# The last two steps of a two-half recurrence: a gate of one half over all four column tiles, and two x units for the second half first

## The chip, the cores and the metric

The kernel runs on one core of one Trainium2 chip. The metric is the device time in microseconds. TensorE (PE in the profile; its weight loads are PEld) has a 128 x 128 array that this kernel uses as four column tiles of 32 columns each; the four tiles work side by side on separate products. VectorE (DVE), ScalarE (ACT), GpSimd (POOL) and SyncE (SP, which here issues DMA transfers) run beside it, each in the order of its own list of instructions, and wait for each other through semaphores.

## The reference

A gated recurrence over T = 128 steps for a batch of 64, with 512 inputs and a state of 512, whose output is added to the input:

```python
comb = concat([x_t, h])
z = sigmoid(comb @ Wz + bz)
r = sigmoid(comb @ Wr + br)
h_cand = tanh(concat([x_t, r * h]) @ Wh + bh)
h_new = (1 - z) * h + z * h_cand
h = tanh(h_new @ Wp + bp) if (t + 1) % 4 == 0 and t < T - 1 else h_new
out[:, t] = x[:, t] + h_new
```

All data is fp32. The part `x_t @ W` does not depend on the state and can be worked out at any time before its step; the part `h @ W` and everything behind it is a chain from step to step.

## The kernel before

**Halves and tiles.** The batch is two halves of 32 (`h` = 0, 1). A gate's 512 results are split by columns in two parts of 256. Half 0 keeps column tiles 0 and 1, half 1 tiles 2 and 3; a tile holds the 32 batches of its half in its 32 columns' partitions and 256 results along the free dimension. The state enters turned, as weights of 128 x 32. `gate` (L255) makes the recurrent product of one gate for one half: K = 4 parts of the 512-long sum, and in `products` (L244, the matmul at L246) one fp32 matmul of 128 x 256 for each of the two tiles. One k of one half and one unit of x work of one half have the same number of columns (256 on each tile of the pair).

**A step** (`half`, one coroutine per half) has gates R, Z and H, and after each fourth step but the last a gate P (the propagation, with `wp`). After R the sigmoid goes to `r_` (`crossed`, L276 to L281: two ACT instructions of 64 rows, since the two parts of a gate lie in two halves of a bank), DVE multiplies by the state (L918) and turns the result (L284): that is the weights of gate H. After Z come sigmoid and `keep` (L941); after H the tanh (L281), z times it (L980), the new state (L993) and its turning (L284): that is the weights of the next R. `r_` (L198) is the last quarter of PSUM bank `scratch_r`.

**Banks.** Three PSUM banks (`rec`) hold the gates; five (`scratch_q`, `_r`, `_a`, `_x`, `_y`) take the x products. `seed` (L439) copies x product and bias into a gate's bank with ACT (L442) before the recurrent product adds to it. For most steps the x products come from a fast matrix scheme with 192-column matmuls (`batch`, L529) whose sums GpSimd puts together; for the first steps and the last two from `plain` (L505), a direct product of twelve units a step, to which DVE adds the bias (`add_bias`, L480 and L483).

**Order.** x work stands in one queue of units (`put`, L454). `fill(n, h)` (L460) runs the next n units of the queue for one half; each half goes through the whole queue at its own place. A unit that writes a bank waits, for half 0, until half 1 has gone past the last unit whose result is read out of that bank; the reading itself (`end`) is issued when half 1 runs the unit. How many units stand after gate Z, after gate H and after gate P of a step is written in `PLACES`, `HEAD` and `TAIL` (L669 to L676, the last by step). The two coroutines are merged by a clock that counts columns (L1019 to L1031): the half that is behind goes next, and half 1 begins 700 columns later (`LAG`).

**The end.** x + h_new is put into `xr` by GpSimd (L876) and sent by SP, every four steps in eight transfers (L886); at step T - 2 the eight transfers hold three steps. The last step adds by DVE (L951, L983); half 0 goes out in one transfer on SP (L985) and half 1 in four, two on SP and two on ACT's queue (L990). `late(t)` names the steps (T - 7 and from T - 5) in which the two halves of Z are activated apart.

Of the kernel before, what the change touches and what calls it, by code (L numbers as in the profile page):

```python
# [13 lines left out]
ALU = mybir.AluOpType  # L14
# [4 lines left out]
def kernel(  # L19
# [417 lines left out]
                G[2 * q + b] = cp[q][:, :, b]  # L437

    def seed(i, t, h):  # L439
        if t < T:  # L440
            rows = slice(None) if i == Z else ts(h, 2 * V)
            nc.scalar.copy(  # L442
                gate_ps(i, h)[rows].rearrange("p d (c n) -> p d c n", c=C),
                G[t][rows, :, :, i, :].rearrange("p c d n -> p d c n"),
            )
# [6 lines left out]
    reader = {}  # L452

    def put(units):  # L454
        for unit, cols, bank, end, read in units:
            queue.append((unit, cols, reader.get(bank, -1), end))
            for b in read:
                reader[b] = len(queue) - 1

    def fill(n, h):  # L460
        for _ in range(n):
            if place[h] == len(queue):
                return
            unit, cols, after, end = queue[place[h]]
            while h == 0 and after >= place[1]:
                yield 0
            unit(h)
            yield cols
            place[h] += 1
            if h == 1 and end is not None:  # L470
                end()

    def banks(t):
        first, second = scratch[:2] if t % 2 == 0 else scratch[2:4]
        if t < 2:
            return first[:, : S * J], second[:, : S * J], scratch[4][:, ts(t, S * J)]
        rooms = (first[:, : S * J], first[:, S * J :], second[:, : S * J])
        return (rooms[0], rooms[2], rooms[1]) if t == T - 1 else rooms

    def add_bias(t, gates):  # L480
        new_cp(t // 2)
# [7 lines left out]
    def plain_unit(t, e, k, start, end=None, gates=()):  # L489
        g, i = divmod(t, Q4)  # L490
        bank = (q_bank, q_bank, r_bank) if t % 2 == 0 else (a_bank, a_bank, x_banks[0])
        if t == T - 1:
            bank = (a_bank, x_banks[0], a_bank)
        second = H_ if t in (1, T - 1) else None if t == 0 else Z
        return (
            lambda h: product(
                banks(t)[e], h, xT[g][:, i], wx[:, :, e, :], k, start and e != second
            ),
            S * J,
            bank[e],  # L500
            end,
            {bank[e] for e in gates},
        )
# [14 lines left out]
        ]  # L518

    MB = {}

# [5 lines left out]
    def batch(n, ms):  # L529
        def runs(ps):  # L530
            return ps.rearrange("p m h (g u) -> p m (h g) u", g=3)

        def unit(h, ps, m, j, e, start):
            g, i = ms[m]
            x_, w_ = terms(i)[e]
            right = factor(w_, j)
            products(
                ps[:, m].rearrange("p d (g u) -> p d g u", g=3),
                h,
                lhs(g, x_, j)[:, ts(h, V)],  # L540
                lambda c: right[:, c::2],
                start and m == 0 and e == 0,
            )
# [36 lines left out]
        def end_q2():  # L580
            nonlocal q2
            q2 = copied("cq", "cq2", q_ps)
            nc.vector.tensor_add(blocks(1, 1), runs(q_ps[:, :nm]), runs(T2[what][:, :nm]))  # L583

        def end_r2():
            nc.vector.tensor_add(blocks(0, 1), runs(r_ps[:, :nm]), runs(q2[:, :nm]))
            nc.vector.tensor_add(blocks(1, 0), runs(x_ps[:, :nm]), runs(q2[:, :nm]))  # L587

        seq = []
        for ps, bank, j, start, end, read in (  # L590
            (a_ps, a_bank, 2, True, None, ()),
            (x_ps, x_bank, 7, True, end_x, (x_bank,)),
            (q_ps, q_bank, 1, True, end_q, (q_bank,)),
            (r_ps, r_bank, 5, True, end_r, (r_bank, a_bank)),
            (x_ps, x_bank, 4, False, None, ()),
            (q_ps, q_bank, 6, False, end_q2, (q_bank,)),
            (r_ps, r_bank, 3, False, end_r2, (r_bank, x_bank)),
        ):
            us = units(ps, j, start)
            seq += [(u, 3 * J // 2, bank, None, ()) for u in us[:-1]]  # L600
            seq.append((us[-1], 3 * J // 2, bank, end, read))
        return seq

    M = {}
# [59 lines left out]
    def pair_right(a, p1, x_, g=1):  # L664
# [96 lines left out]
    def begin(t):  # L761
# [54 lines left out]
    def behind_step(t, duo, u, h_new):  # L816
# [78 lines left out]
        if duo >= 0:  # L895
            if u == 3:
                load_xs(odd + 2)
            elif u == 7:
                load_xs(even + 4)

    def half(h):

        for t in range(T):
# [4 lines left out]
            places = HEAD.get(t) or TAIL.get(t) or PLACES[u]  # L908
            if h == 0:
                begin(t)  # L910
            h_old, hT = state[t]

            yield from gate(R, h, hT, wh[R])
# [20 lines left out]

            def gate_z(part, halves, h_old=h_old, z_=z_, keep=keep):
                for i in halves:
                    crossed(z_[:, i, :], i, Z, AF.Sigmoid, not last)
                kept = keep[:, part, :], z_[:, part, :], h_old[:, part, :]
                if last:
                    kept = plain_order(kept[0]), plain_order(kept[1]), state_order(kept[2])  # L940
                nc.vector.scalar_tensor_tensor(  # L941
                    out=kept[0],
                    in0=kept[1],
# [2 lines left out]
                    op0=ALU.subtract,  # L946
                    op1=ALU.mult,
                )
                if last:
                    o = xr[g][:, j, part, :]  # L950
                    nc.vector.tensor_sub(o, o, keep[:, part, :])  # L951

            if h == 1:
                if late(t):
                    gate_z(0, (0,))
                    if last:
                        gate_z(1, (1,))
                else:
                    gate_z(slice(0, S), range(S))
                join(t, duo, u, 1)  # L960
# [15 lines left out]
            if late(t) and h == 1 and not last:  # L976
                gate_z(1, (1,))
            crossed(cand[:, h, :], h, H_, AF.Tanh, not last)
            c = z_[:, h, :]
            nc.vector.tensor_mul(c, cand[:, h, :], c)  # L980
            if last:
                o = xr[g][:, j, h, :]
                nc.vector.tensor_add(o, c, o)  # L983
                if h == 0:
                    nc.sync.dma_start(  # L985
                        out=out[ts(h, V), t, :].rearrange("b (q n) -> q b n", q=NQ), in_=o
                    )
                else:
                    for q in (0, 2, 1, 3):
                        both_queues[q // 2].dma_start(out=out[ts(h, V), t, ts(q, J)], in_=o[part(q)])  # L990
                return
            hT = new_turned("hT", "hT", t)
            nc.vector.tensor_sub(h_new[:, h, :], c, keep[:, h, :])  # L993
            turn(hT[:, h, :], h_new[:, h, :])
            if prop:
                nc.scalar.copy(gate_ps(P_, h)[ts(h, 2 * V)], bias_p[ts(h, 2 * V)])
            elif not late(t + 1):
# [73 lines left out]
```

## Time and profile before

| what | value |
|---|---|
| median of three runs | 1259.13 us (1259.06 to 1259.54) |
| the profiled execution's own time | 1258.66 us |
| its span, first to last instruction | 1256.6 us |
| granted TensorE clock | 1.000 |
| TensorE busy | 1248.4 us (99%), 25952 MATMULs |
| weight loads busy | 1155.6 us (92%) |
| VectorE, ScalarE, GpSimd busy | 809.1, 836.3, 909.7 us (64%, 67%, 72%) |
| HBM | 40.38 MB read, 16.78 MB written, 45 GB/s |

In the rows below, a group is named by its line, engine and operation, then out <- in by the program's names, the shapes and the number of instructions. In a timeline a row has the start in us, the length in us and, in brackets, the idle time of the engine before it and what ended it. The records of matmuls overlap: a record is longer than the distance to the next matmul on the same tile, and the busy time of TensorE counts the stretch that at least one record covers. Each fp32 matmul is recorded as two MATMULs and two LDWEIGHTS.

### The profile page before, as it was taken

Reading aid. Unit: us, or ns where it says so; the run is one execution under the profiler, and the core shown is the slowest. Engines: PE = TensorE matmul, PEld = TensorE weight load, DVE = VectorE, ACT = ScalarE, POOL = GpSimd, SP = SyncE. Lnnn points to the kernel's source line nnn. Section 1 sums busy time; section 2 is a strip of 40 time slices with the busy share of each in tenths; the row PEclk is TensorE's granted clock in tenths of the full one; section 3 lists DMA queues with packets and bytes.
Section 4 is the critical chain, followed back from the end, with each engine's and each line's share of the span. In section 5 each row is a group of like instructions: output and inputs, shape, how many; then the busy total and the mean of one; then the engine's idle time right before and its main releaser. Section 6 shows DMA issues by size and latency. Waiting matters only on the chain.

```text
span 1256.6 us, 60732 instructions
## 1 busy us (share of the span) xinstructions
PE 1248.4 (99%) x25952; PEld 1155.6 (92%) x25952; DVE 809.1 (64%) x2183; ACT 836.3 (67%) x2687; POOL 909.7 (72%) x1032
## 2 busy tenths in 40 slices
PE   9999999999999999999999999999999999999998
PEld 5899999999999999999999999999999999999975
DVE  5666666666666666666666666666666666666554
ACT  2566666666666676666666666666676666666665
POOL 4988777777876788767777677787777787677530
PEclk9999999999999999999999999999999999999999
DMA  7311212121122120121111211111211112111011
GB/s 244 96 32 43 52 36 53 39 52 41 32 53 50 40 52 22 51 54 37 53 30 44 52 47 43 41 46 39 53 37 49 40 37 54 45 45 36 13 37 25
DMA packets 112290, 61.09 MB, mean 49 GB/s; under 512 B 12777, under 2 KB 109301, under 8 KB 112021
## 3 DMA queue, kind: packets, MB, share of 16 engines
q1 hardware_dynamic: 111588, 56.90, 17.0%
q8 instruction: 205, 3.36, 1.2%
q14 instruction: 65, 0.52, 0.1%
q0 software_dynamic: 256, 0.14, 0.1%
q10 hardware_dynamic: 176, 0.16, 0.1%
HBM read 40.38 MB, written 16.78 MB: 45 GB/s over the span
## 4 chain that ended last, share of the span: by engine, by line
PE 98%; DMA 1%; issue 1%; SPq 0%; DVE 0%; POOLq 0%; POOL 0%; ACT 0%; ACTq 0%
PE rec L246 45%; PE rec_z L246 16%; PE scratch_r L246 14%; PE scratch_q L246 11%; PE scratch_a L246 5%; PE scratch_y L246 4%; PE scratch_x L246 4%; DMA wx<-in_L_cond_Wr_dram 0%; SPq L886 0%; DMA out_dram<-xr 0%; SPq L127 0%; POOLq L1066 0%; POOL xr L876 0%; DVE z L980 0%; SPq L141 0%
## 5 line engine op out<-in xcount | busy, mean ns | idle before, releaser
L246 PE MATMUL rec<-wh,rhT 128*32 128x256 f32 x4096 | 376.6, 379 | 0.0
L246 PE MATMUL rec<-wh,hT 128*32 128x256 f32 x3072 | 282.9, 379 | 0.0
L246 PE MATMUL rec_z<-wh,hT 128*32 128x256 f32 x3072 | 282.8, 379 | 0.0
L246 PEld LDWEIGHTS rec<-wh,rhT 128*32 128x32 f32 x4096 | 248.5, 110 | 22.3 <-ACT rec L442 1.2
L281 ACT ACTIVATE scratch_r<-rec 64x128 f32<-64x128 f32 x512 | 128.0, 250 | 132.9 <-PE rec L246 65.3
L442 ACT COPY rec<-cp 64x256 f32<-64x256 f32 x512 | 189.9, 371 | 20.2 <-DVE cp L483 0.3
L246 PEld LDWEIGHTS rec<-wh,hT 128*32 128x32 f32 x3072 | 186.7, 110 | 16.2 <-issue 1.9
L246 PEld LDWEIGHTS rec_z<-wh,hT 128*32 128x32 f32 x3072 | 193.3, 110 | 8.1
L281 ACT ACTIVATE rec_z<-rec_z 64x128 f32<-64x128 f32 x488 | 122.0, 250 | 91.1 <-PE rec_z L246 79.2
L281 ACT ACTIVATE c<-rec 64x128 f32<-64x128 f32 x512 | 138.8, 271 | 60.7 <-PE rec L246 48.8
L876 POOL TENSOR_TENSOR xr<-xr,h 128x256 f32<-128x256 f32 x125 | 109.4, 876 | 85.3 <-DVE h L993 83.0
L621 POOL TENSOR_TENSOR cp<-mb,mb 128x768 f32<-128x768 f32 x76 | 139.2, 1831 | 9.3 <-DVE mb L587 5.7
L621 POOL TENSOR_TENSOR mb<-mb,mb 128x768 f32<-128x768 f32 x58 | 106.3, 1833 | 45.5 <-DVE mb L587 45.5
L621 POOL TENSOR_TENSOR cp<-mb 128x768 f32<-128x768 f32 x46 | 84.3, 1832 | 56.9 <-ACT rec_z L442 55.5
L246 PE MATMUL scratch_r<-tw,s 128*32 128x192 f32 x928 | 120.8, 326 | 0.0
L560 ACT COPY cq<-scratch_q 128x384 f32<-128x384 f32 x212 | 102.0, 481 | 19.2 <-PE scratch_q L246 17.7
L577 DVE TENSOR_TENSOR cx<-scratch_r,cx 128x384 f32<-128x384 f32 x106 | 59.1, 557 | 84.1 <-PE scratch_r L246 68.8
L246 PE MATMUL scratch_q<-tt,s 128*32 128x192 f32 x928 | 103.5, 326 | 0.0
L941 DVE SCALAR_TENSOR_TENSOR keep<-rec_z,h 128x256 f32<-128x256 f32 x91 | 38.6, 425 | 94.8 <-ACT rec_z L281 87.4
L583 DVE TENSOR_TENSOR mb<-scratch_q,cx 128x384 f32<-128x384 f32 x106 | 59.1, 558 | 62.4 <-ACT cq L560 62.4
L918 DVE TENSOR_TENSOR rh<-scratch_r,h 128x128 f32<-128x128 f32 x192 | 56.0, 292 | 61.2 <-ACT scratch_r L281 61.2
L246 PE MATMUL rec<-wp,hT 128*32 128x256 f32 x992 | 91.6, 379 | 0.1
(207 smaller groups left out, 3851.0 us busy)
## 6 DMA issues: line engine op xcount, KB each, us to landing
out_dram<-xr SPq DMA_DIRECT2D x249, 64.0 KB, 1.8
xr<-in_x_dram SPq DMA_DIRECT2D x248, 64.0 KB, 2.3
xs<-in_x_dram SPq DMA_DIRECT2D x240, 64.0 KB, 2.1
wx<-in_L_cond_Wz_dram SPq DMA_DIRECT2D x2, 512.0 KB, 7.8
wx<-in_L_cond_Wh_dram SPq DMA_DIRECT2D x2, 512.0 KB, 9.1
wh<-in_L_cond_Wr_dram SPq DMA_DIRECT2D x2, 512.0 KB, 7.7
wh<-in_L_cond_Wz_dram SPq DMA_DIRECT2D x2, 512.0 KB, 5.7
wh<-in_L_cond_Wh_dram SPq DMA_DIRECT2D x2, 512.0 KB, 9.4
```

What stands on the lines that cost most here:

```text
L246: nc.tensor.matmul(ps[part(2 * h + c)], lhsT=left, rhs=rhs(c), start=start, stop=True, skip_group_check=True,)
L281: nc.scalar.activation(o, v, func)
L442: nc.scalar.copy(gate_ps(i, h)[rows].rearrange("p d (c n) -> p d c n", c=C), G[t][rows, :, :, i, :].rearrange("p c d n -> p d c n"),)
L560: nc.scalar.copy(c[:, :nm], ps[:, :nm])
L577: nc.vector.tensor_add(T2[what][:, :nm], r_ps[:, :nm], T2[what][:, :nm])
L583: nc.vector.tensor_add(blocks(1, 1), runs(q_ps[:, :nm]), runs(T2[what][:, :nm]))
L621: nc.gpsimd.tensor_add(dst, a, b)
L876: nc.gpsimd.tensor_add(o, o, h_new.rearrange("p h (k e) -> p h e k", k=K))
L918: nc.vector.tensor_mul(rh[:, h, :], r_, h_old[:, h, :])
L941: nc.vector.scalar_tensor_tensor(out=kept[0], in0=kept[1], scalar=1.0, in1=kept[2], op0=ALU.subtract, op1=ALU.mult,)
```

## The change

**Two units first.** Half 1 begins 188 columns after half 0 and runs two units of the x queue before its first gate (`AHEAD`), so its gates begin 188 + 2 x 256 = 700 columns after half 0's as before, while its x units stand nearer to half 0's. Since now either half may be the first at a unit, `fill` makes either one wait for the other's place, a unit can name several banks, and `end` is issued by whichever half is later.

**The last two steps** (`WIDE`) go through `wide_step`. Here the coroutines are two lanes: lane 0 has column tiles 0 and 1, lane 1 tiles 2 and 3. A gate of one half is made by both lanes: each tile holds 128 of the 512 results of the 32 batches, in fp32 matmuls of 128 columns, four k on each of the four tiles. The gates of the two halves follow one another in the order R0, Z0, R1, H0, Z1, H1. Their x products are `wide_unit`s (24 in all, of four matmuls a lane) and their biases are twelve small bf16 matmuls of a lane and step (`wide_bias`), and both go straight into the banks in which the gates are summed: q and r at step T - 2, a and x at T - 1. So there is no seeding copy and no adding of biases for these two steps, and one ACT instruction of 128 rows serves a gate where there were two of 64. The x units of these steps are drawn forward by `TAIL`: all are run by the end of step T - 3.

```diff
     def seed(i, t, h):
-        if t < T:
+        if t < T - WIDE:
...
     def put(units):
-        for unit, cols, bank, end, read in units:
-            queue.append((unit, cols, reader.get(bank, -1), end))
+        for unit, cols, used, end, read in units:
+            after = max(reader.get(b, -1) for b in used)
+            queue.append((unit, cols, after, end))
...
-            while h == 0 and after >= place[1]:
+            while after >= place[1 - h]:
                 yield 0
             unit(h)
             yield cols
             place[h] += 1
-            if h == 1 and end is not None:
+            if place[1 - h] >= place[h] and end is not None:
                 end()
...
+    ORDER = ((R, 0), (Z, 0), (R, 1), (H_, 0), (Z, 1), (H_, 1))
+
+    def wide_bank(t):
+        return a_bank if t == T - 1 else q_bank
+
+    def wide(t, i, h):
+        n, bank = divmod(ORDER.index((i, h)), 2)
+        return scratch[wide_bank(t) + bank][:, ts(n, J)]
+
+    def wide_products(t, i, h, lane, left, w, start=False):
+        for c in range(2):
+            q = 2 * lane + c
+            nc.tensor.matmul(
+                wide(t, i, h)[part(q)],
+                lhsT=left,
+                rhs=w[:, ts(q, J)],
+                start=start,
+                stop=True,
+                skip_group_check=True,
+            )
+
+    def wide_gate(t, i, h, lane, lT, w):
+        for k in range(K):
+            wide_products(t, i, h, lane, lT[:, h, ts(k, V)], w[:, k])
+            yield S * J // 2
+
+    def wide_unit(t, i, k):
+        g, j = divmod(t, Q4)
+        c0, s0 = divmod(k, C)
+
+        def unit(lane):
+            for h in range(S):
+                left = xT[g][:, j][:, c0, s0 * B + h * V : s0 * B + (h + 1) * V]
+                wide_products(t, i, h, lane, left, wx[:, k, i], i != H_ and h == 0 and k == 0)
+
+        return unit, S * J, {wide_bank(t), wide_bank(t) + 1}, None, ()
+
+    def wide_bias(t, lane):
+        for i, row in ((R, 0), (H_, 1), (Z, 2)):
+            for h in range(S):
+                for c in range(2):
+                    q = 2 * lane + c
+                    nc.tensor.matmul(
+                        wide(t, i, h)[part(q)],
+                        lhsT=picks[:, q],
+                        rhs=thirds[:, row],
...
     TAIL = {
-        T - 10: (6, 8, 0), T - 9: (1, 7, 5), T - 8: (1, 7, 0), T - 7: (0, 6, 0), T - 6: (0, 5, 0),
-        T - 5: (0, 4, 3), T - 4: (0, 4, 0), T - 3: (0, 4, 0), T - 2: (0, 5, 0), T - 1: (0, 0, 0),
+        T - 10: (6, 8, 0), T - 9: (1, 7, 5), T - 8: (1, 7, 0), T - 7: (0, 6, 0), T - 6: (1, 5, 0),
+        T - 5: (0, 5, 3), T - 4: (1, 5, 0), T - 3: (1, 5, 0), T - 2: (0, 0, 0), T - 1: (0, 0, 0),
     }
+
+    AHEAD = 2
+    WIDE = 2
...
-                + plain(T - 1, (R,))[:2]
-                + plain(T - 2)
-                + plain(T - 1, (R,))[2:]
-                + plain(T - 1, (Z,))
-                + plain(T - 1, (H_,))
+                + [wide_unit(T - n, i, k) for n in (2, 1) for i in (R, Z, H_) for k in range(K)]
...
+    def wide_step(t, lane):
...
+        wide_bias(t, lane)
+        for i, h in ORDER:
+            yield from until(t, H_ if i == H_ else None, h)
+            yield from wide_gate(t, i, h, lane, rhT if i == H_ else hT, wh[i])
+            if lane == 0:
+                continue
+            v, o = wide(t, i, h), xr[g][:, j, h, :]
+            if not last:
+                v = plain_order(v)
+            if i == R:
+                nc.scalar.activation(state_order(r_), plain_order(wide(t, i, h)), AF.Sigmoid)
+                nc.vector.tensor_mul(rh[:, h, :], r_, h_old[:, h, :])
+                turn(rhT[:, h, :], rh[:, h, :])
+                made_by.add((t, H_, h))
...
+            if t >= T - WIDE:
+                yield from wide_step(t, h)
+                if last:
+                    return
+                if h == 1:
+                    behind_step(t, duo, u, state[t + 1][0])
+                continue
+            if t == 0 and h == 1:
+                yield from fill(AHEAD, h)
...
-    LAG = 700
+    LAG = 188
...
         elif cost == 0:
-            at[1] += next(halves[1], 0)
+            at[1 - h] += next(halves[1 - h], 0)
```

More of the change, by code (lines that the diff above doesn't have):

```diff
@@ L491, in plain_unit @@
         bank = (q_bank, q_bank, r_bank) if t % 2 == 0 else (a_bank, a_bank, x_banks[0])
[L492 to L494 removed]
+        second = H_ if t == 1 else None if t == 0 else Z
         return (
@@ L499, in plain_unit @@
             S * J,
-            bank[e],
+            {bank[e]},
             end,
@@ L599, in batch @@
             us = units(ps, j, start)
-            seq += [(u, 3 * J // 2, bank, None, ()) for u in us[:-1]]
-            seq.append((us[-1], 3 * J // 2, bank, end, read))
+            seq += [(u, 3 * J // 2, {bank}, None, ()) for u in us[:-1]]
+            seq.append((us[-1], 3 * J // 2, {bank}, end, read))
         return seq
@@ L899, in behind_step, with until @@
                 load_xs(even + 4)
+    made_by = set()
+    def until(*what):
+        while what not in made_by:
+            yield 0
+    def wide_step(t, lane):
+        g, j = divmod(t, Q4)
+        last = t == T - 1
+        rh, rhT = new_two("rh", t), new_turned("rhT", "rhT", t)
+        cand, keep = new_two("c", t), new_two("keep", t)
+        z_ = shared(t, "z", lambda: one.tile([P, S, J], F32, tag="o12", name=f"z_{t}"))
+        h_new, hT_new = (None, None) if last else (new_two("h", t), new_turned("hT", "hT", t))
+        h_old, hT = state[t]
+        state[t + 1] = h_new, hT_new
+        yield from fill(AT_LAST[t][lane], lane)
+        wide_bias(t, lane)
[12 more added lines that the diff above has]
+                made_by.add((t, H_, h))
+            elif i == Z:
+                z_h, kept, h_h = z_[:, h, :], keep[:, h, :], h_old[:, h, :]
+                nc.scalar.activation(z_h if last else state_order(z_h), v, AF.Sigmoid)
+                if last:
+                    kept, z_h, h_h = plain_order(kept), plain_order(z_h), state_order(h_h)
+                nc.vector.scalar_tensor_tensor(
+                    out=kept, in0=z_h, scalar=1.0, in1=h_h, op0=ALU.subtract, op1=ALU.mult
+                )
+                if last:
+                    nc.vector.tensor_sub(o, o, keep[:, h, :])
+            else:
+                c, z_h = cand[:, h, :], z_[:, h, :]
+                nc.scalar.activation(c if last else state_order(c), v, AF.Tanh)
+                nc.vector.tensor_mul(z_h, c, z_h)
+                if not last:
+                    nc.vector.tensor_sub(h_new[:, h, :], z_h, keep[:, h, :])
+                    turn(hT_new[:, h, :], h_new[:, h, :])
+                    made_by.add((t + 1, None, h))
+                    continue
+                nc.vector.tensor_add(o, z_h, o)
+                if h == 0:
+                    nc.sync.dma_start(
+                        out=out[ts(h, V), t, :].rearrange("b (q n) -> q b n", q=NQ), in_=o
+                    )
+                else:
+                    for q in (0, 2, 1, 3):
+                        both_queues[q // 2].dma_start(out=out[ts(h, V), t, ts(q, J)], in_=o[part(q)])
@@ L975, in half @@
             cand = new_two("c", t)
-            if late(t) and h == 1 and not last:
+            if late(t) and h == 1:
                 gate_z(1, (1,))
-            crossed(cand[:, h, :], h, H_, AF.Tanh, not last)
+            crossed(cand[:, h, :], h, H_, AF.Tanh)
             c = z_[:, h, :]
             nc.vector.tensor_mul(c, cand[:, h, :], c)
[L981 to L991, printed above, removed]
             hT = new_turned("hT", "hT", t)
```

21 lines of the change are left out of this document (11 added, 10 removed).

## The prediction

> **What bounds the kernel now.** I read the page's parts 1 and 4, then the groups by line, then the timeline wherever TensorE is released by something. First the page: busy time, the chain that ended last, and three groups with their mean times.
>
> ```profile
> PE 1248.4 (99%) x25952; PEld 1155.6 (92%) x25952; DVE 809.1 (64%) x2183; ACT 836.3 (67%) x2687; POOL 909.7 (72%) x1032
> PE 98%; DMA 1%; issue 1%; SPq 0%; DVE 0%; POOLq 0%; POOL 0%; ACT 0%; ACTq 0%
> L246 PE MATMUL rec<-wh,rhT 128*32 128x256 f32 x4096 | 376.6, 379 | 0.0
> L246 PE MATMUL scratch_r<-tw,s 128*32 128x192 f32 x928 | 120.8, 326 | 0.0
> L246 PEld LDWEIGHTS rec<-wh,rhT 128*32 128x32 f32 x4096 | 248.5, 110 | 22.3 <-ACT rec L442 1.2
> ```
>
> TensorE is 98% of the chain; every other engine has a quarter of its time free. So the sum is one of TensorE's work and TensorE's waits. A fp32 matmul stands in the trace as two MATMULs, and the four column tiles run side by side. The next rows show one tile pair stepping.
>
> ```profile
> 1219.12 0.41 PE L246 MATMUL rec<-wp,hT 128*32 128x256 f32 x2
> 1219.33 0.41 PE L246 MATMUL rec<-wp,hT 128*32 128x256 f32 x2
> 1219.55 0.41 PE L246 MATMUL rec<-wp,hT 128*32 128x256 f32 x2
> 12.71 0.29 PE L217 MATMUL scratch_a<-thirds,picks 96*32 96x128 bf16 x8
> 12.82 1.05 PE L246 MATMUL scratch_r<-wx,xT 128*32 128x256 f32 x16
> ```
>
> The starts are 0.2155 us apart: one slot of a 256-column MATMUL on its tile (the record is longer than the slot, 0.38 to 0.41). A unit of x or one k of a gate (two slots) is 0.431, a gate of four k 1.724. A 192-column record is 53 ns shorter than a 256-column one for 64 columns less; so I take 0.2155 - 2 x 0.053 = 0.109 us for a 128-column slot, which does not occur before. Eight bf16 MATMULs of 128 columns, two on each tile, went in 12.82 - 12.71 = 0.11, so 0.055 each.
>
> Around the changed steps TensorE does wait. Two windows (us, busy and count for PE, PEld, DVE, ACT, POOL, then clock, DMA share, GB/s), then five places where it stood:
>
> ```profile
> 1205.00:1236.80 31.80, 31.73 (x558) 22.16 (x557) 16.26 (x53) 20.81 (x72) 10.66 (x8) 1.00 0.08 19
> 1236.80:1250.50 13.70, 13.70 (x236) 10.38 (x232) 7.32 (x25) 8.67 (x31) 1.73 (x2) 1.00 0.12 30
> 1207.68 0.14 PEld L246 LDWEIGHTS rec<-wh,rhT 128*32 128x32 f32 x3 [0.33 <-ACT scratch_r L281]
> 1218.87 0.14 PEld L246 LDWEIGHTS rec<-wp,hT 128*32 128x32 f32 x3 [0.51 <-ACT z L281]
> 1229.41 0.14 PEld L246 LDWEIGHTS rec<-wh,hT 128*32 128x32 f32 x3 [0.24 <-issue]
> 1229.44 0.41 PE L246 MATMUL rec<-wh,hT 128*32 128x256 f32 x2
> 1234.36 0.36 PEld L246 LDWEIGHTS rec<-wh,rhT 128*32 128x32 f32 x10 [0.36 <-ACT rec L442]
> 1236.83 0.41 PE L246 MATMUL rec<-wh,hT 128*32 128x256 f32 x2
> ```
>
> Four tiles at full rate take one MATMUL per 0.2155 / 4 = 0.0539 us. So 558 are 30.07 us and the first window loses 1.73; 236 are 12.72 and the second loses 0.98. The clock is 1.00 in both.
>
> **The change, part by part.** The end is reached by each tile pair through its own list; I follow pair A (tiles 0, 1; half 0 before, lane 0 after).
>
> (1) x work of the last two steps is drawn forward. By the end of gate H of step T-3, lane 0 has run 6 + 8 + 6 + 1 = 21 units after the change and 5 + 7 + 4 = 16 before. Five more, though 24 units are done in all as before: 5 x 0.431 = **+2.16**. (A new unit is four 128-column matmuls of a lane, two on each tile, four slots of 0.109: the same columns.)
>
> (2) These units stand where TensorE waited. The wait ahead of T-2 (0.28, from the rows below) stays, since its chain does not change, and I leave 0.20 of small rest: 1.73 - 0.28 - 0.20 = **-1.25**. Bounds: all of the window's loss, -1.73, and half of the four released stalls shown (0.33 + 0.51 + 0.24 + 0.36 = 1.44, which TensorE's loads show for both pairs together), -0.72, if units cover one pair alone.
>
> The chain between gate H and the next gate R, here of T-2 to T-1, and that between R and H:
>
> ```profile
> 1243.57 0.56 ACT L281 ACTIVATE c<-rec 64x128 f32<-64x128 f32 x2
> 1242.93 0.29 DVE L980 TENSOR_TENSOR z<-c,z 128x128 f32<-128x128 f32 x1 [0.28 <-ACT c L281]
> 1243.33 0.29 DVE L993 TENSOR_TENSOR h<-z,keep 128x128 f32<-128x128 f32 x1
> 1243.65 0.31 DVE L284 STREAM_TRANSPOSE hT<-h 128x128 f32<-128x128 f32 x1
> 1244.08 0.14 PEld L246 LDWEIGHTS rec<-wh,hT 128*32 128x32 f32 x3 [0.24 <-issue]
> 1246.07 0.53 ACT L281 ACTIVATE scratch_r<-rec 64x128 f32<-64x128 f32 x2 [1.54 <-PE rec L246]
> 1246.63 0.29 DVE L918 TENSOR_TENSOR rh<-scratch_r,h 128x128 f32<-128x128 f32 x1 [0.97 <-ACT scratch_r L281]
> 1246.96 0.31 DVE L284 STREAM_TRANSPOSE rhT<-rh 128x128 f32<-128x128 f32 x1
> ```
>
> From the first DVE operation to the load 1244.08 - 1242.93 = 1.15; with both activations (0.55), 0.03 between and 0.26 from the slot's end to the activation (at the end of the run, part 4: 1250.56 to 1250.82) it is 1.99. Four units cover 1.72 of it: a wait of about 0.28 remains ahead of T-2. After, lane 0 has only three units and its biases there; the chain sets the start either way, so nothing is gained or lost from H of T-3 to R of T-2.
>
> (3) From that R to TensorE's end. Before: 1236.83 to 1250.56 (0.2155 after the last MATMUL's start, 1250.34), 13.73 (rows in part 4). After: a gate of one half is 4 k x 2 slots x 0.109 = 0.87 on all four tiles, six gates to a step: 2 x 5.22 = 10.45 instead of 2 x 3 x 1.724 = 10.34. Biases: 12 bf16 matmuls of a lane and step, 6 on each tile, 6 x 0.055 = 0.33; only lane 1's lie on the path, twice: 0.66 (lane 0's lie in waits).
>
> Then the waits. In T-2 the gates' banks are q and r, and the sigmoid of R is written into the last quarter of bank r (L198). In the changed program's order the sigmoid of R0 waits for lane 0's first half of Z0, which is written into bank r, and lane 1's first product of Z0 waits until rh is multiplied. TensorE takes its instructions in order, so both lanes stand behind that wait: 0.26 + one activation 0.27 + 0.04 + multiply 0.29 + about 0.1 = 0.96, and again at R1 against H0: 2 x 0.98 = 1.96 with the lanes' offset. No row before shows such a wait; bounds: nothing if lane 0's early half were to fill it (0), and 2 x 1.31 if it lasts to the end of the transpose (1246.07 to 1247.38, when the load of H's product is issued). In T-1 the banks are a and x and this does not occur; but each gate reuses the bank of the gate before the last, 0.87 - 0.33 = 0.54 after that one's end, and an activation needs 0.26 + 0.27 + 0.08 = 0.61: 4 x 0.07 = 0.3 more. T-2 is 5.22 + 0.33 + 1.96 = 7.51, T-1 5.22 + 0.33 + 0.3 = 5.85; together 13.36, so **-0.37**.
>
> The Trainium skill, *PSUM — Partial Sum Buffer*, "PSUM bank collisions raise a hardware error", says that two engines may not touch the same bank in the same 32 partitions at once and that the chip does not hold them apart itself. By that rule these two waits cannot be avoided by columns alone, only by another bank; no run yet shows them.
>
> (4) After TensorE's end: the last tanh, sums and output.
>
> ```profile
> 1250.09 0.63 PE L246 MATMUL rec<-wh,rhT 128*32 128x256 f32 x4
> 1250.82 0.27 ACT L281 ACTIVATE c<-rec 64x128 f32<-64x128 f32 x1
> 1251.10 0.27 ACT L281 ACTIVATE c<-rec 64x128 f32<-64x128 f32 x1
> 1251.41 0.29 DVE L980 TENSOR_TENSOR z<-c,z 128x128 f32<-128x128 f32 x1
> 1251.73 0.29 DVE L983 TENSOR_TENSOR xr<-z,xr 128x128 f32<-128x128 f32 x1
> 1251.52 0.69 SPq L985 DMA_DIRECT2D out_dram<-xr  x1
> 1252.06 1.54 ACTq L990 DMA_DIRECT2D out_dram<-xr  x2
> 1252.32 1.41 SPq L990 DMA_DIRECT2D out_dram<-xr  x2
> 1245.83 3.62 SPq L886 DMA_DIRECT2D out_dram<-xr  x8
> ```
>
> The last record ends at 1250.72 and is 0.38 long (379 ns in its group), so it began at 1250.34. One activation of 128 rows replaces two of 64; the second began 0.285 after the first: **-0.29**. SP was held by half 0's output until 1252.21, past the ACT queue's 1252.06; half 0 now ends a gate earlier, and the two queues can start together: **-0.10**. The eight outputs of T-2 need 3.6 us of SP, from about 9.7 to 13.4 us after the start of T-2; they are through just before half 0's output. If not, up to 0.3 comes back.
>
> (5) What costs nothing: the copies that seed the banks and the DVE adds of the bias fall away for two steps; both engines had time, so their absence gives nothing outside the chain. The bounds are 0 and -0.4 (one copy of 64x256 is 0.37).
>
> (6) Two units first for half 1, and a start 188 columns behind instead of 700. The distance of the gates stays 700 columns (188 + 2 x 256); the x units of the lanes come closer in TensorE's order, and so each bank is read and freed sooner. In the middle TensorE waits little: 100 us there show it busy throughout, and the waits that records overlap are those between a 192-column slot and gate H, 604.18 - 603.91 - 0.16 = 0.11 here and two of some 0.14 in each 8 steps by the starts.
>
> ```profile
> 300.00:400.00 100.00, 100.00 (x2115) 94.86 (x2109) 65.77 (x176) 68.83 (x220) 73.37 (x87) 1.00 0.18 45
> 603.91 0.33 PE L246 MATMUL scratch_a<-wx,xT 128*32 128x192 f32 x1
> 604.18 0.41 PE L246 MATMUL rec<-wh,rhT 128*32 128x256 f32 x2
> ```
>
> I take 0; bounds 15 x 0.14 = 2.1 us either way, averaged over the tiles, when these waits go or double.
>
> Sum: 2.16 - 1.25 - 0.37 - 0.29 - 0.10 = **+0.15** on the profiled 1258.66, 1258.81. That execution (its span is 1256.6, with 2.1 around it) is 0.47 under the median 1259.13 of three runs, so I predict **1259.3**. A measurement of this kernel tells about 0.2%, 2.5 us, from no change.
>
> **The rivals.** *Slower, by small products.* A 128-column slot must also hold its weight load (110 ns). If a load's last 0.031 us can't overlap (after the stall at 1229.41 the MATMUL starts that long after its load), a slot is 0.141 instead of 0.109; with 192 such slots on each tile that is +6.2, 1265.5. It passes 2.5 us from a slot of 0.121. For it: the load is as long as the slot. Against: in the rows at 12.71 a tile took a load and a MATMUL every 0.055. Chance 0.07. The Trainium skill, *TensorE: Matmul & The Clock Gate*, "Back-to-back issue gap", gives about 81 ns for a load and a matmul of 128 columns where the columns alone would give 56; were those 25 ns added to each slot, an estimate is 192 x 0.025 = 4.8 and 1264. The rows at 12.71 speak against that on one tile of four.
>
> *Faster, by the middle and the bank waits.* If the two waits in T-2 cost nothing, -1.96 and 1257.4; if the middle loses its waits, -2.1 and 1257.3. Each alone stays within 2.5 us of the median; both give 1255.3. For the first: lane 0 already has work ahead of lane 1; against: the order puts the wait ahead of that work. Chance 0.10.
>
> *Slower, in the middle.* The copies that free x banks now stand ahead of other work on ACT; if each 8 steps lose 0.3, 15 x 0.3 = 4.5 and 1263.9. ACT is 67% busy and the waits there are short. Chance 0.04.
>
> *The units ahead do nothing:* both halves run the same list of units, so two of half 1's drawn ahead are two fewer behind, and where TensorE never waits no order is better. Then (6) is exactly 0, and the time is the forecast's; its chance lies in that of the forecast.
>
> **How the numbers follow.** The forecast has 0.79, with its own bounds 1257.2 to 1261.4: below, the T-2 waits gone; above, 0.5 in (2), 0.7 in (3), 0.3 each of SP and of the T-1 waits doubled, and a little of (6). The faster rival has 0.10, the slower ones 0.07 and 0.04. So faster 0.10, same 0.79, slower 0.11. The range takes in the part of the middle's loss that is small: 1257.0 to 1262.0. Left out are the faster rival, the small products and half of the middle's loss, 0.10 + 0.07 + 0.02 = 0.19.
>
> **What would show it.** Right: rows of 128 columns 0.109 apart; two stalls of about 1 us in T-2 released by rh's multiply; no stall over 0.2 from T-6 to T-3; one tanh of 128 rows after TensorE's end. Wrong: 128-column slots over 0.12; a middle window with fewer MATMULs; x work that waits for its banks in T-4 or T-3.

## The result, and the profile after

The changed kernel takes 1311.68 us in the median of five runs (1310.5 to 1312.18), the kernel before 1259.13. The ratio is 1.0415, with a 95% interval of 1.0404 to 1.0427: 52 us slower. The prediction was 1259.3 with a range of 1257.0 to 1262.0.

The page of the changed kernel, busy times and the chain that ended last:

```profile
PE 1265.5 (97%) x26384; PEld 1043.2 (80%) x26384; DVE 808.3 (62%) x2177; ACT 832.8 (64%) x2665; POOL 909.1 (69%) x1032
PE 79%; ACT 11%; DVE 8%; issue 2%; DMA 1%; POOL 0%; SPq 0%; DVEq 0%; ACTq 0%; POOLq 0%
```

TensorE's share of the chain falls from 98% to 79%, and ScalarE and VectorE, which had none of it, have 11% and 8%. The work is nearly the same, so TensorE now waits for them. Where? A window in the middle (columns as in the prediction):

```profile
300.00:400.00 100.00, 97.34 (x2014) 81.03 (x2010) 62.84 (x169) 66.12 (x211) 75.00 (x86) 1.00 0.17 43
```

It held 2115 MATMULs before and holds 2014 now, 4.8% fewer, at the same clock of 1.00. The loss is spread over the whole kernel, far from the two steps that were rewritten. The view of waits names it (engine, what waited, for whom: us in total, times, longest):

```profile
PEld scratch_x L246 <- ACT cx L609: 24.8, 30, 1.2
PEld scratch_y L246 <- ACT cx L609: 24.2, 30, 1.0
PEld scratch_q L246 <- DVE mb L632: 13.2, 14, 0.9
PE scratch_x L246 <- ACT cx L609: 12.7, 30, 0.7
PE scratch_y L246 <- ACT cx L609: 12.3, 30, 0.6
PE scratch_q L246 <- DVE mb L632: 6.5, 14, 0.5
```

74 times TensorE stood before it could write a bank of x products again, because the copy out of it (`cx`, by ScalarE) or a sum from it was late. Its loads stood 62.2 us, its matmuls at least 31.5; the loss lies between. In the kernel before no wait of that kind stands in this view. One cycle of 8 steps in the timeline, from the first row below to the last, is 80.23 us long (the last row is the same place one cycle on, with banks x and y exchanged), against 76.88 in the kernel before (488.79 to 565.67 there): 3.35 lost, in 15 cycles 50. The five waits behind the first row belong to it:

```profile
505.71 0.11 PEld L246 LDWEIGHTS scratch_y<-tt,xT 128*32 128x32 f32 x2 [0.65 <-ACT cx L609]
514.92 0.11 PEld L246 LDWEIGHTS scratch_q<-tw,o 128*32 128x32 f32 x2 [0.94 <-DVE mb L632]
553.25 0.11 PEld L246 LDWEIGHTS scratch_y<-tt,xT 128*32 128x32 f32 x2 [0.96 <-ACT cx L609]
565.54 0.11 PEld L246 LDWEIGHTS scratch_x<-tt,o 128*32 128x32 f32 x2 [1.01 <-ACT cx L609]
575.74 0.11 PEld L246 LDWEIGHTS scratch_y<-tt,o 128*32 128x32 f32 x2 [0.65 <-ACT cx L609]
585.94 0.11 PEld L246 LDWEIGHTS scratch_x<-tt,xT 128*32 128x32 f32 x2 [0.65 <-ACT cx L609]
```

Around the wait at 575.74, ScalarE's list and bank y in the changed kernel:

```profile
573.56 0.56 ACT L281 ACTIVATE c<-rec 64x128 f32<-64x128 f32 x2
573.83 0.33 PE L246 MATMUL scratch_y<-tt,s 128*32 128x192 f32 x2
574.15 0.37 ACT L442 COPY rec<-cp 64x256 f32<-64x256 f32 x1
574.81 0.38 ACT L442 COPY rec_z<-cp 128x256 f32<-128x256 f32 x1 [0.29 <-DVE h L1091]
575.21 0.48 ACT L609 COPY cx<-scratch_y 128x384 f32<-128x384 f32 x1
575.74 0.36 PE L246 MATMUL scratch_y<-tt,o 128*32 128x192 f32 x2 [0.26 <-ACT cx L609]
```

The last product into bank y is complete at 574.16, and `cx` needs nothing else. But it is the fourth in ScalarE's list: ahead of it stand half 1's tanh, the seed of its next gate H, and the seed of the next gate Z, which itself waits 0.29 until VectorE has made the new state. So `cx` begins at 575.21, over 1 us late, and TensorE, which has come to the next write of bank y, stands until 575.74. The same place in the kernel before:

```profile
551.14 0.56 ACT L281 ACTIVATE c<-rec 64x128 f32<-64x128 f32 x2
552.04 0.36 PE L246 MATMUL scratch_y<-tt,s 128*32 128x192 f32 x2
552.38 0.38 ACT L442 COPY rec_z<-cp 128x256 f32<-128x256 f32 x1 [0.28 <-DVE h L993]
552.79 0.48 ACT L560 COPY cx<-scratch_y 128x384 f32<-128x384 f32 x1
555.08 1.22 PE L246 MATMUL rec_z<-wh,hT 128*32 128x256 f32 x16
555.94 0.36 PE L246 MATMUL scratch_y<-tt,o 128*32 128x192 f32 x2
531.92 0.48 ACT L560 COPY cx<-scratch_y 128x384 f32<-128x384 f32 x1
533.03 0.36 PE L246 MATMUL scratch_y<-tt,xT 128*32 128x192 f32 x2
```

There too `cx` comes behind the tanh and the Z seed. But the last product began 0.90 after the tanh (551.14 to 552.04) and now begins 0.27 after it (573.56 to 573.83), about two units sooner, so that `cx`, which the list holds back, began 0.39 after that product's end before and 1.05 after the change. And the bank was written again 3.9 us after the last product began (552.04 to 555.94), so that the copy ended 555.94 - 553.27 = 2.67 ahead; after the change it is 1.9 with the wait in it. At the tightest place of this cycle before (the last two rows) the copy ended 533.03 - 532.40 = 0.63 ahead of the next write. That place waits after the change. So do three whose copies had 2.3, 2.7 and 2.7 us to spare, while two with 0.82 (ahead of 511.70 and 521.43) do not.

### The profile page after: what moved, and what is told of

Read it like the earlier page. It is cut to its first block, busy times and chain, and to the rows that moved or that the text cites. A ratio compares the mean times of both kernels' runs of the same rounds, so it can differ in the third digit from the quotient of the medians.

```text
span 1308.6 us, 61433 instructions
## 1 busy us (share of the span) xinstructions
PE 1265.5 (97%) x26384; PEld 1043.2 (80%) x26384; DVE 808.3 (62%) x2177; ACT 832.8 (64%) x2665; POOL 909.1 (69%) x1032
## 4 chain that ended last, share of the span: by engine, by line
PE 79%; ACT 11%; DVE 8%; issue 2%; DMA 1%; POOL 0%; SPq 0%; DVEq 0%; ACTq 0%; POOLq 0%
PE rec L246 35%; PE rec_z L246 16%; PE scratch_r L246 7%; PE scratch_q L246 7%; PE scratch_a L246 4%; PE scratch_y L246 4%; PE scratch_x L246 4%; ACT c L281 3%; DVE h L1091 3%; DVE rec_z L1089 3%; ACT rec_z L281 2%; ACT cx L609 2%; ACT rec_z L442 2%; DVE hT L284 1%; DVE mb L632 1%
## 5 line engine op out<-in xcount | busy, mean ns | idle before, releaser
L246 PE MATMUL rec<-wh,hT 128*32 128x256 f32 x3008 | 291.6, 380 | 0.0
L246 PEld LDWEIGHTS rec<-wh,rhT 128*32 128x32 f32 x4032 | 213.0, 110 | 32.1 <-ACT rec L442 0.3
L442 ACT COPY rec<-cp 64x256 f32<-64x256 f32 x504 | 186.9, 371 | 19.4 <-DVE cp L483 0.2
L246 PEld LDWEIGHTS rec_z<-wh,hT 128*32 128x32 f32 x3008 | 158.3, 110 | 28.2
L246 PEld LDWEIGHTS rec<-wh,hT 128*32 128x32 f32 x3008 | 151.0, 110 | 32.2 <-ACT rec_z L442 0.2
L670 POOL TENSOR_TENSOR cp<-mb,mb 128x768 f32<-128x768 f32 x76 | 139.3, 1833 | 10.1 <-DVE mb L636 6.4
L246 PE MATMUL scratch_r<-tw,s 128*32 128x192 f32 x928 | 109.3, 326 | 0.0
L246 PE MATMUL rec<-wp,hT 128*32 128x256 f32 x992 | 99.6, 381 | 0.0
L246 PE MATMUL rec<-wh,hpT 128*32 128x256 f32 x992 | 93.8, 379 | 0.0
L246 PE MATMUL rec_z<-wh,hpT 128*32 128x256 f32 x992 | 93.6, 379 | 0.0
L1089 DVE TENSOR_TENSOR rec_z<-c,rec_z 128x128 f32<-128x128 f32 x244 | 72.2, 296 | 34.6 <-ACT c L281 24.4
```

What stands on the lines that cost most here:

```text
L246: nc.tensor.matmul(ps[part(2 * h + c)], lhsT=left, rhs=rhs(c), start=start, stop=True, skip_group_check=True,)
L442: nc.scalar.copy(gate_ps(i, h)[rows].rearrange("p d (c n) -> p d c n", c=C), G[t][rows, :, :, i, :].rearrange("p c d n -> p d c n"),)
L670: nc.gpsimd.tensor_add(dst, a, b)
```

## The experiments

**The wide last steps without the units ahead.**

```diff
-    AHEAD = 2
+    AHEAD = 0
...
-    LAG = 188
+    LAG = 700
```

> The change without its first part: no x units ahead for half 1, start 700 columns behind as before; the last two steps are wide as in the changed kernel. Theory A (the loss comes from the two units ahead: half 1 writes an x bank again two units sooner, while the copy that frees it is given to ScalarE behind the seed of gate Z): the middle is as before and the time is 1259 to 1260, by the sum of parts 1 to 5 of the prediction 1259.3. Theory B (the small products of the last two steps or the new placing of units in the last steps cost it): more than 1300 remains. The profile of the changed kernel speaks for A, since each 100 us of its middle hold some 90 MATMULs fewer.

Measured: 1263.35 us, ratio 1.0039 (1.0025 to 1.0052). 48 of the 52 us are gone, so the units ahead made them: theory A. But 4.4 remain, where the sum of the other parts had given nothing. Its waits in the two wide steps, from the first gate R of T-2:

```profile
1237.35 0.14 PEld L532 LDWEIGHTS scratch_q<-wh,hT 128*32 128x32 f32 x3 [0.32 <-DVE hT L284]
1240.42 0.11 PEld L532 LDWEIGHTS scratch_r<-wh,hT 128*32 128x32 f32 x2 [0.96 <-DVE rh L977]
...
1243.71 0.11 PEld L532 LDWEIGHTS scratch_r<-wh,rhT 128*32 128x32 f32 x2 [1.01 <-DVE rh L977]
1246.26 0.11 PEld L532 LDWEIGHTS scratch_a<-wh,hT 128*32 128x32 f32 x2 [0.27 <-DVE hT L284]
1248.95 0.25 PEld L532 LDWEIGHTS scratch_a<-wh,hT 128*32 128x32 f32 x10 [0.67 <-DVE hT L284]
...
1251.68 0.11 PEld L532 LDWEIGHTS scratch_x<-wh,rhT 128*32 128x32 f32 x2 [0.63 <-ACT z L982]
...
```

T-2 takes 1246.26 - 1237.35 = 8.9 us and T-1 10.1. Besides the two waits for rh that were foretold there are waits of 0.6 to 0.7 at nearly each gate of T-1. The two lanes here are 700 columns apart in TensorE's list, over five k of a wide gate's 128 columns. A gate is complete only when the later lane has done it; the earlier one stands at the gate behind, and, the list being taken in order, holds up the later one too. This reading is tried below, under "The lanes meet".

**The units ahead without the wide steps.** The kernel before, with these lines:

```diff
-            while h == 0 and after >= place[1]:
+            while after >= place[1 - h]:
...
-            if h == 1 and end is not None:
+            if place[1 - h] >= place[h] and end is not None:
...
+            if t == 0 and h == 1:
+                yield from fill(2, h)
...
-    LAG = 700
+    LAG = 188
...
-            at[1] += next(halves[1], 0)
+            at[1 - h] += next(halves[1 - h], 0)
```

> The kernel before with the first part alone: two x units ahead for half 1, start 188 columns behind, either half waits for the other and the later one issues the reading; last steps as before. Theory A: 3.26 us lost in each 8 steps (80.23 against 76.97), 15 times, so 1259 + 49 = 1308, between 1304 and 1312. Theory B: 1259, within 3.

Measured: 1309.76 us, 1.0405 (1.0386 to 1.0424), 50.8 more than its own reference runs (1258.98). The first part alone brings the loss, with the same waits, of which one row:

```profile
PEld scratch_x L246 <- ACT cx L560: 24.9, 30, 1.2
```

**One step moved in ScalarE's list.** The changed kernel, with half 1's seed of gate Z behind its first two units instead of ahead:

```diff
-            if h == 1:
-                seed(Z, t + 1, 0)
             state[t + 1] = h_new, hT
-            yield from fill(places[1], h)
+            if h == 1:
+                yield from fill(2, h)
+                seed(Z, t + 1, 0)
+            yield from fill(places[1] - 2 * h, h)
```

> The changed kernel with one step moved: half 1 issues the seed of the next gate Z after its first two units behind gate H instead of ahead of them, so that the copies out of the x banks no longer stand behind it in ScalarE's list. Theory A1 (the wait of that seed for the state's subtraction, 0.28, and its own 0.38, hold up the copy): the four waits for cx of 0.65 to 1.0 in 8 steps become 0 to 0.35; about 2.0 to 2.6 of the 3.26 us come back, 1270 to 1280. Theory A2 (the bank is simply wanted two units too early, whatever ScalarE's order): 1305 to 1312.

Measured: 1268.0 us, 1.0074 (1.006 to 1.0087), against 1311.68 of the changed kernel. No unit was moved and no work taken away, only one copy of 0.38 us in ScalarE's list, and 43.7 us came back, more than A1 said. Its timeline at the place shown above:

```profile
556.44 0.33 PE L246 MATMUL scratch_y<-tt,s 128*32 128x192 f32 x2
556.76 0.37 ACT L442 COPY rec<-cp 64x256 f32<-64x256 f32 x1
557.16 0.48 ACT L609 COPY cx<-scratch_y 128x384 f32<-128x384 f32 x1
557.66 0.38 ACT L442 COPY rec_z<-cp 128x256 f32<-128x256 f32 x1
557.90 0.33 PE L246 MATMUL scratch_y<-tt,o 128*32 128x192 f32 x2
```

`cx` begins 0.39 after the last product and ends at 557.64, ahead of the next write; the Z seed follows it, and no longer waits for the state.

As nothing waits at this place any more, its rows show how far the next write moved: it begins 1.46 behind the last product (556.44 to 557.90), 2.44 sooner than before the change, where two units of 192 columns are only 0.65 (four slots of 0.16). The program's order of instructions says why. Before, half 0 came first to this unit, behind its gates R and Z of the next step (the last products of gate Z are in the row at 555.08). Now it is one of the two that half 1 runs ahead, and half 1 comes to it first, ahead of its own gate R. Of the 2.67 us that the copy had to spare 0.26 are left, and in the changed kernel the copy's later start used up more than that.

**One unit ahead.**

```diff
-    AHEAD = 2
+    AHEAD = 1
...
-    LAG = 188
+    LAG = 444
```

> The changed kernel with one unit ahead and a start 444 columns behind, so that the gates stay 700 apart. Theory A1 or A2: a 192-column unit of a half and its pair is 0.32 us; the waits of 0.65 to 1.0 become 0.33 to 0.7, so roughly half of the 50 us, 1275 to 1295. A rival (that half 1 is ahead at all changes the order of the copies, not by how much): 1305 to 1312.

Measured: 1288.66 us, 1.0238 (1.0219 to 1.0256): 29.7 lost, where the changed kernel with two units ahead lost 52.5. The rival falls: the loss grows with the distance by which half 1 is ahead, so when a bank's last product and its next write come counts besides the order of the copies.

**Both seeds moved.** As two experiments before, and half 1's seed of gate H too:

```diff
-            elif not late(t + 1):
+            elif not late(t + 1) and h == 0:
                 seed(H_, t + 1, h)
...
                 yield from fill(2, h)
+                if not prop and not late(t + 1):
+                    seed(H_, t + 1, h)
                 seed(Z, t + 1, 0)
```

> As e3_z_seed_later, and half 1's seed of the next gate H also goes behind its first two units (not at steps with a propagation, where the copy of that gate's bias stays). In e3_z_seed_later the copy out of the x bank still stands behind this seed, 0.37 us, and TensorE still waits 0.36 for it at five places in 8 steps at most. Theory A1 (the place of the copy in ScalarE's list is the cause of the rest too): most of the 7.4 us that the middle of e3_z_seed_later lost against the kernel before come back, 1260.5 to 1264. Theory A2 (the rest is the bank wanted too early): 1266.5 to 1268.5.

Measured: 1264.02 us, 1.0046 (1.0031 to 1.0061), at the upper edge of A1. In its view of waits

```profile
PEld scratch_q L246 <- DVE mb L632: 4.0, 14, 0.3
PEld scratch_y L246 <- ACT cx L609: 3.2, 8, 0.6
PEld scratch_x L246 <- ACT cx L609: 2.5, 7, 0.4
```

remain: for the copy 15, which is one in each 8 steps, and for the sum 14, one in each 8 steps too. The one for the copy comes at a step with a propagation, where the copy of the propagation's bias still stands ahead of it. That these waits are the 5 us that are left was not tried.

**The lanes meet.** Now the last steps by themselves. As in the first experiment, but the 700 columns end where the wide steps begin:

```diff
         yield from fill(AT_LAST[t][lane], lane)
+        if t == T - WIDE:
+            made_by.add(("here", lane))
+            while lane == 0 and ("here", 1) not in made_by:
+                yield 0
+            if lane == 0:
+                at[0] = at[1] - 0
         wide_bias(t, lane)
```

> The wide last steps without units ahead, as in e1_wide_alone, but lane 0 waits at the first wide step until lane 1 has come there, and both go on from the same place of the column clock (the 700 columns between them end there). Theory C (e1_wide_alone was 4.4 us slower than the kernel before because its lanes run about three k apart, so that each wait of one stands in front of the other's matmuls: T-2 and T-1 took 8.90 and 10.11 us there, and 7.69 and 5.96 in the changed kernel, whose lanes are closer): T-2 and T-1 fall to about 7.7 and 6.0, at most 0.5 is paid for the meeting, 1258.0 to 1259.3. Rival D (the five units drawn ahead of T-2 or the wide products themselves cost the 4.4): 1262.5 to 1264.

Measured: 1259.89 us, 1.0009 (1.0000 to 1.0018), above the number expected but far from rival D. T-2 and T-1 took 7.7 and 5.5 us instead of 8.9 and 10.1, so theory C holds. Two things were priced too low. T-2 begins at 1238.25, 0.9 later than in the first experiment. And from TensorE's end to the end of the span it takes 6.3 us instead of 5.0: SP's last transfers now begin 1.3 behind ACT's, after the eight of T-2, which the last experiment takes up. In the two wide steps only the foretold waits are left:

```profile
1240.26 0.81 PEld L532 LDWEIGHTS scratch_r<-wh,hT 128*32 128x32 f32 x32 [0.96 <-DVE rh L983]
1242.98 0.81 PEld L532 LDWEIGHTS scratch_r<-wh,rhT 128*32 128x32 f32 x32 [1.04 <-DVE rh L983]
```

**Another bank for T-2.** In addition, the gates of T-2 in banks q and y:

```diff
-    def wide_bank(t):
-        return a_bank if t == T - 1 else q_bank
+    def wide_banks(t):
+        return (a_bank, x_banks[0]) if t == T - 1 else (q_bank, x_banks[1])
...
-        return scratch[wide_bank(t) + bank][:, ts(n, J)]
+        return scratch[wide_banks(t)[bank]][:, ts(n, J)]
...
```

> As e6_lanes_meet, and the gates of T-2 use the banks q and y in place of q and r, so that the sigmoid of R, which is written into bank r, shares no bank with a gate. By part 3 of the prediction the two waits of T-2 (0.85 to 1.1 in the changed kernel's trace) go: T-2 falls from 7.7 by 1.2 to 2.0, 1256.3 to 1257.6. Rival: H0 and H1 then wait for their turned rh, which was hidden behind those waits (sigmoid, multiply, transpose, 1.0), and only 0 to 0.8 is gained.

Measured: 1257.72 us, 0.9990 (0.9981 to 0.9999). T-2 takes 5.6 us, 2.1 less; both waits are gone and rh's chain stays hidden behind gate Z. This is the first version a little faster than the kernel before, with an interval that ends just under 1.

**Biases first.** Lane 0 issues `wide_bias` ahead of the meeting.

> As e7_lanes_meet_y, but lane 0 issues its biases of a wide step before it waits for lane 1. In the trace of e7_lanes_meet_y both pairs of tiles stand 1.5 us around the meeting and lane 0's biases come after it. If they lie on the path there, 0.1 to 0.3 is gained in T-2 (1257.4 to 1257.6, within the noise); if lane 1's own list sets the start, nothing.

Measured: 1257.81 us, 0.9992 (0.9983 to 1.0001): no difference from the one above that the noise would let one see. In its trace lane 0's biases begin at 1237.38, and the first gate only at 1238.88, behind lane 1's biases (from 1238.62), so lane 1's list sets the start of T-2.

**The last outputs.** In addition:

```diff
-            n = 3 if t == T - 2 else 0
+            n = {T - 3: 2, T - 2: 1}.get(t, 0)
...
-            for h in range(S):
+            for h in range(1 if t == T - 2 else S):
...
-                        both_queues[q // 2].dma_start(out=out[ts(h, V), t, ts(q, J)], in_=o[part(q)])
+                        both_queues[q // 2].dma_start(
+                            out=out[ts(h, V), t - 1 : t + 1, ts(q, J)],
+                            in_=xr[g][part(q), j - 1 : j + 1, h, :],
+                        )
```

> As e8_bias_first, and the outputs of the last four steps go out otherwise: steps T-4 and T-3 at T-3, half 0 of T-2 at T-2 (four transfers in place of eight), and half 1 of T-2 together with T-1 in the four last transfers. In e7_lanes_meet_y the eight transfers of T-2 hold SP until half 0's last output begins at 1251.47, 0.3 after half 1's sum starts, and SP's last two begin 0.8 us behind ACT's; the time from TensorE's end to the end is 5.99 there and 4.96 in e1_wide_alone, where SP was free. If SP is what is late, 0.6 to 1.0 is gained on e8_bias_first, 1256.8 to 1257.2. If the landing of the transfers sets the end, nothing.

Measured: 1255.91 us against 1258.06 of the kernel before in the same series, 0.9980 (0.9971 to 0.9989), the fastest of all. The DMA rows of the end, of the kernel with biases first and then of this one:

```profile
1251.22 0.83 ACTq L1015 DMA_DIRECT2D out_dram<-xr  x2
1251.91 0.83 SPq L1015 DMA_DIRECT2D out_dram<-xr  x2
```

```profile
1250.85 0.80 SPq L1015 DMA_DIRECT2D out_dram<-xr  x2
1250.89 0.84 ACTq L1015 DMA_DIRECT2D out_dram<-xr  x2
```

SP's last transfers no longer begin 0.7 after ACT's, and from TensorE's end to the end of the span it takes 4.45 us instead of 5.93. Each against its own reference runs, this kernel gains 2.15 and the one with biases first 1.14: 1.0 more, the upper end of what was expected if SP is late. (The median itself is under the 1256.8 to 1257.2 expected, since the reference runs of this series are 0.9 faster.)

## Why the prediction was wrong

The step that failed is **(6)**, the two units first: "I take 0; bounds 15 x 0.14 = 2.1 us either way". The runs show 50.8 for it alone. The bound was made from TensorE's waits in the kernel before, and these say how much there was to win, not how much there was to lose: a change that lets a bank be wanted earlier can make a wait where none stood. The reason given, "each bank is read and freed sooner", was wrong. A bank's last product came sooner, by two units, but not its reading, which in ScalarE's list stands behind half 1's tanh and seeds as before. And the next write came sooner by more than two units, since half 1 runs it ahead of its gate R where half 0 had run it behind gates R and Z: 2.44 us at the place shown, out of 2.67 to spare. The order of the changed program and the rows of the kernel before held both.

The rival "slower, in the middle" had the mechanism half right (the copies out of the x banks, in ScalarE's list, in each 8 steps), but put them ahead of other work, where they stand behind it, priced them at 0.3 a cycle instead of some 3.4, and got a chance of 0.04. The argument against it, that ScalarE is only 67% busy, has no weight in a list that is taken in order: it was free for work, and the copy could not get at it behind a seed that waited for VectorE.

The other points, in the trace of the changed kernel. Gates of T-2 and T-1 there, the first waits, and the end:

```profile
1289.38 0.28 PE L532 MATMUL scratch_q<-wh,hT 128*32 128x128 f32 x2
1289.49 0.28 PE L532 MATMUL scratch_q<-wh,hT 128*32 128x128 f32 x2
1291.44 0.47 PEld L532 LDWEIGHTS scratch_r<-wh,hT 128*32 128x32 f32 x18 [0.95 <-DVE rh L977]
1294.26 0.25 PEld L532 LDWEIGHTS scratch_r<-wh,rhT 128*32 128x32 f32 x9 [1.01 <-DVE rh L977]
1296.94 0.28 PE L532 MATMUL scratch_a<-wh,hT 128*32 128x128 f32 x2
1303.11 0.28 ACT L992 ACTIVATE c<-scratch_x 128x128 f32<-128x128 f32 x1 [0.83 <-PE scratch_x L532]
1303.64 0.69 SPq L1001 DMA_DIRECT2D out_dram<-xr  x1
1304.07 1.02 ACTq L1006 DMA_DIRECT2D out_dram<-xr  x2
1304.44 0.83 SPq L1006 DMA_DIRECT2D out_dram<-xr  x2
```

- (1) to (5) together were to cost +0.15. The changed kernel lost 52.5 and the two units alone 50.8, so they cost some 1.8.
- (1) and (2), units drawn forward, waits covered: +0.91 net was predicted for the start of T-2. It began at 1237.35 in the kernel with the wide steps alone, against 1236.83, +0.5; of the stalls from T-6 to T-3 only one of 0.20 is left there. About right. In the changed kernel itself one more came, a wait of up to 1.9 us at the turn from T-7 to T-6, where the first unit into bank q waits for a late sum of the same kind as in the middle.
- (3), T-2 and T-1: 7.51 and 5.85 were predicted; 7.69 (1289.25 to 1296.94) and 5.96 came, 13.65 against 13.73 before. The slot of a 128-column product is 0.11 as estimated, and the two waits in T-2 are 0.95 and 1.01 against 0.96 to 0.98. They last to the end of rh's multiplication, not to that of the transpose. What the step did not say is that these numbers hold only while the lanes are close: at 700 columns apart the same work takes 19.0. So the start 188 columns behind, which with the units ahead cost 50.8, saved about 5 in the last two steps.
- The two waits were put down to the bank that the sigmoid of R shares with a gate. With bank y in place of r both went, and 2.1 us with them. The Trainium skill, *PSUM — Partial Sum Buffer*, "PSUM bank collisions raise a hardware error", says that two engines may not touch the same bank in the same 32 partitions at once. The runs agree with it as far as they go.
- (4), the end: -0.29 for one tanh and -0.10 for SP. The first output of ACT's queue began 1.17 after TensorE's last slot (1302.90 to 1304.07) against 1.50 before, so that the first half is right. SP was late after all, at 1304.44: the eight transfers of T-2 were to be through 13.4 us after its start, ran until 14.3 (1303.54), and half 0's output began behind them. From TensorE's last slot to the end of the span it took 5.75 us against 5.99, 0.24 less instead of 0.39.
- (5), copies and adds that fall away: no run tries them by themselves.
- The rival "slower, by small products" fell: a slot is 0.11, half of one of 256 columns, with its load in it. The Trainium skill, *TensorE: Matmul & The Clock Gate*, "Back-to-back issue gap", gives about 81 ns for a load and a matmul of 128 columns, against 56 for the columns alone. The 25 ns more, which the prediction's estimate added to each slot, did not come.
- The rival "faster" asked for both the waits of T-2 and those of the middle to go. The first part came only with another bank, the second not at all.

## What to carry to other kernels

Where the busiest engine is at 100%, ask of a reordering what it can newly make late. For each buffer that is written again, take from the trace the time between the end of its read-out and the next write, and work out from the program's order how far the change brings that write forward: not only by the units that are moved, but by all the work that they now pass, here two gates. Then read the list of the engine that does the read-out: one instruction that waits, issued a few places ahead, holds up every later one however idle the engine is. And two streams that share an in-order engine and meet at each step should run close together; if they must be kept apart elsewhere, let them meet where the dependence begins.

## What the runs showed of the hardware that was not expected

With its own load before each, a fp32 MATMUL of 128 columns went every 0.109 us, half a 256-column slot (1289.38 to 1289.49 in the rows above). T-2 of the kernel with bank y shows it for all four tiles: its 48 such slots and lane 1's biases of 0.33 make 5.56 us, and it took 5.60. A load is recorded with 110 ns, as long as the slot, so it must lie beside matmuls and not between them. And a stalled TensorE went on about 0.05 us after the copy that it waited for (575.69 to 575.74), so a wait for a bank costs little beyond the lateness itself.
